# Attentions 1 and 2 of a four-layer decoder: values of both query tiles at once, a pair of jobs later; scores in pieces of 400 columns

## The chip, the cores and the metric

The kernel runs on one core of a Trainium2 chip. The metric is the device time of one execution in microseconds; the table below gives the median of three runs. One execution was also recorded by the hardware profiler, and every duration in this text is read from that record. The engines are TensorE (PE, with its weight loads listed apart as PEld), VectorE (DVE), ScalarE (ACT), GpSimd (POOL) and SyncE (SP, which starts DMAs). Each engine works through its own queue in the order written; engines wait for one another through semaphores.

## The reference

The model takes eight batches of 256 tokens with 128 features, `x`, and for each batch a context of 1601 rows with 64 features. Four layers follow, each a cross attention on the context and a feed-forward block:

```python
x = x + _L0_xattn_ref(_layernorm(x), ctx, ctx, ...)
x = x + _L0_ffn_ref(_layernorm(x), ...)
x = x + _L1_xattn_ref(_layernorm(x), ctx, ...)      # 16 heads of 64
x = x + _L1_ffn_ref(_layernorm(x), ...)
x = x + _L2_xattn_ref(_layernorm(x), ctx, ctx, ...)  # one head
...
scores = jnp.einsum('bhnd,bhmd->bhnm', qh, kh) * scale
attn = jax.nn.softmax(scores, axis=-1)
out = jnp.einsum('bhnm,bhmd->bhnd', attn, vh)
out = out.transpose(0, 2, 1, 3).reshape(B, N, INNER)
return out @ Wo + bo
```

The change touches only the attentions of layers 1 and 2 (counted from 0). Both are computed by one function with the key weights folded into the queries and the value and output weights folded into one matrix per head, so that the context itself, transposed, serves as the keys and, as it is, as the values.

## The kernel before

The function `wide` runs attentions 1 and 2. Its unit is a *job*: one layer and batch, one head `h`, and one tile `j` of 128 queries (0 or 1; `QT` is 2). Attention 1 has 8 batches x 16 heads x 2 tiles = 256 jobs, attention 2 has 8 x 1 x 2 = 16. Jobs 2p and 2p+1 are the two query tiles of one head; this text calls them *pair* p, its even and its odd job.

One job n goes through these steps, with the lines of the profile:

- `scores` (L467): the 128 queries against the 1601 context columns, in four pieces of 512, 512, 512 and 66 columns (65 are used), each piece two matmuls (`qh` and `ql`, the high and low parts of the queries, in the type fp32r). Each piece has its own bank of the accumulator memory PSUM; there are four such banks (`s=4`).
- `maximum` (L474, L477), on VectorE: the maximum of each piece and then of the row. `exponentials` (L488), on ScalarE: four exponentials with sums, which free the four banks, into `e`.
- `turn` (L500, L502): `e` is transposed on TensorE in 13 chunks of 128 columns (the last has 65), four chunks to a turn, into one of two banks (`t=2`), and copied to a tile `pt`. Turns 0 and 1 are copied by ScalarE, turns 2 and 3 by VectorE.
- `values` (L514): 13 fp32 matmuls of the context chunk (64 columns of weights) with the turned chunk (128 moving columns). Even chunks write partitions 0 to 63 of the bank `o` and odd chunks 64 to 127; an fp32 matmul is two instructions in the profile, so 26 are listed a job. There is one bank `o` (`o=1`).
- `take` (L524), on ScalarE, copies the result out, `project` (L528) multiplies it with the output matrix of the head into other columns of the same bank, and `add` (L532), on VectorE, scales it by the inverse sum (`sums`, L519, L520) and adds it to `X[b]`.
- `query` (L438, L443, L444) makes the queries of the next head; it is called in odd jobs.

The order is written out by hand: the body of the loop over n is emitted as it stands, and every engine gets its own instructions in that order. Around job n it is: scores and maxima of job n+1; turns 0 and 1 of job n; project and add of job n-1; now and then a layer norm for a later batch; in odd jobs the queries of the next head; the exponentials of job n+1; turns 2 and 3 of job n; its sums; a step `EARLY` of other work; values and take of job n; a step `LATE` of other work. The other work ("beside") is the feed-forward blocks of layers 0 and 1 for other batches and the preparation of weights, cut into steps of which most jobs get one. `EARLY` issues a step's TensorE, first ScalarE and VectorE parts, `LATE` its other ScalarE and GpSimd parts.

Of the kernel before, what the change touches and what calls it, by code (L numbers as in the profile page):

```python
# [33 lines left out]
F32 = mybir.dt.float32  # L34
F32R = mybir.dt.float32r
AF = mybir.ActivationFunctionType
ALU = mybir.AluOpType
AX = mybir.AxisListType

P = 128  # L40
D = 128
DC = 64
NB = 8
LQ = 256
QT = LQ // P
LK = 1601
NC = (LK + P - 1) // P
LAST = LK - (NC - 1) * P
MAGIC = 12582912.0
TAKEN = -3.0e38  # L50
KW = LK + 1
# [6 lines left out]
def decoder_kernel(ctx: ExitStack, tc: tile.TileContext, a: dict, out: bass.AP):  # L58
    nc = tc.nc
# [18 lines left out]
    def pm():  # L78
        return ps["m"].tile([P, 512], F32, tag="m", name="pm")

    def po():
        return ps["o"].tile([P, 512], F32, tag="o", name="o")
# [63 lines left out]
    X = [const.tile([P, QT, D], F32, tag=f"x{b}", name=f"x{b}") for b in range(NB)]  # L146
# [200 lines left out]
    def run(steps, names):  # L347
        for name in names:
            for step in steps:
                if name in step:  # L350
                    step[name]()
# [38 lines left out]
    def wide(layers, before, extra):  # L390
# [11 lines left out]
        with ExitStack() as es:  # L402
            one = es.enter_context(tc.tile_pool(name="wi1", bufs=1))
            two = es.enter_context(tc.tile_pool(name="wi2", bufs=2))
# [3 lines left out]
            B = [one.tile([P, n, D], F32, name=f"B{l}") for l, (n, _) in enumerate(layers)]  # L408
            bias = {}
            ct, v, y, yT, q, own = {}, {}, {}, {}, {}, {}  # L410

            def load_batch(k):
                ct[k] = two.tile([P, KW], F32R, tag="ct", name="ct")
                nc.sync.dma_start(out=ct[k].bitcast(F32), in_=ctd[k[1]])
                v[k] = two.tile([P, NC, DC], F32, tag="v", name="v")
                load_context(v[k], k[1])
# [6 lines left out]
            def measure(k):  # L423
                stats[k] = deviation(two, k[1])

            def start_batch(k):
                l, b = k
                y[k] = normalise(two, b, *stats[k])
                nc.gpsimd.tensor_tensor(X[b], X[b], layers[l][1][:, None, :].to_broadcast([P, QT, D]), ALU.add)

            def turn_y(k):
                yT[k] = flip_tokens(two, y[k], "yT")
# [24 lines left out]
            jobs = [(k, h, j) for k in keys for h in range(layers[k[0]][0]) for j in range(QT)]  # L457
            st, e, ls, tail = {}, {}, {}, {}

            BANK = [(at, min(512, LK - at)) for at in range(0, LK, 512)]  # L460

            def scores(n, c):
                k, h, j = jobs[n]
                st[n, c] = ps["s"].tile([P, 512], F32, tag="s", name="st")
                at, w = 512 * c, min(512, KW - 512 * c)
                for i in range(2):
                    nc.tensor.matmul(st[n, c][:, 0:w], lhsT=q[k, h][i][:, j * P:(j + 1) * P],  # L467
                                     rhs=ct[k][:, at:at + w], start=(i == 0), stop=(i == 1))

            def maximum(n, c):  # L470

                if c == 0:
                    ls[n] = two.tile([P, 12], F32, tag="ls", name="ls", bufs=3)
                nc.vector.tensor_reduce(ls[n][:, c:c + 1], st[n, c][:, 0:BANK[c][1]], AX.X, ALU.max)  # L474
                if c == 3:
                    shift = ls[n][:, 4:5]
                    nc.vector.tensor_reduce(shift, ls[n][:, 0:4], AX.X, ALU.max, negate=True)  # L477
                    k, _, j = jobs[n]
                    if k[0] in bias:

                        c = own[k][:, j:j + 1]
                        nc.vector.tensor_tensor(shift, shift, c, ALU.subtract)
                        nc.vector.tensor_tensor(shift, shift, c, ALU.add)

            def exponentials(n):
                e[n] = two.tile([P, LK], F32, tag="e", name="e")
                for c, (at, w) in enumerate(BANK):
                    nc.scalar.activation(e[n][:, at:at + w], st[n, c][:, 0:w], AF.Exp, bias=ls[n][:, 4:5], scale=1.0,  # L488
                                         accum_out=ls[n][:, 5 + c:6 + c])

            turned = {}

            def turn(n, i):

                t = ps["t"].tile([P, 512], F32, tag="t", name="t")
                p = turned[n, i] = two.tile([P, 512], F32, tag="pt", name="pt", bufs=5)
                cs = range(4 * i, min(4 * i + 4, NC))
                m = P if cs[-1] < NC - 1 else LAST
                for c in cs:
                    nc.tensor.transpose(t[0:m, (c - 4 * i) * P:(c - 4 * i + 1) * P], e[n][:, c * P:c * P + m], ident)  # L500
                w = P * len(cs)
                (nc.scalar.copy if i < 2 else nc.vector.tensor_copy)(p[0:m, 0:w], t[0:m, 0:w])  # L502

            o = {}

            def values(n, cs):

                k, h, j = jobs[n]
                if cs[0] == 0:
                    o[n] = po()  # L510
                for c in cs:
                    m = P if c < NC - 1 else LAST
                    half = slice(DC * (c % 2), DC * (c % 2) + DC)
                    nc.tensor.matmul(o[n][half, 0:P], lhsT=v[k][0:m, c, :],  # L514
                                     rhs=turned[n, c // 4][0:m, (c % 4) * P:(c % 4 + 1) * P],
                                     start=(c < 2), stop=(c >= NC - 2))

            def sums(n):
                nc.vector.tensor_reduce(ls[n][:, 9:10], ls[n][:, 5:9], AX.X, ALU.add)  # L519
                nc.vector.reciprocal(ls[n][:, 9:10], ls[n][:, 9:10])  # L520

            def take(n):
                tail[n] = two.tile([P, P], F32, tag="os", name="os")
                nc.scalar.copy(tail[n], o[n][:, 0:P])  # L524

            def project(n):
                (l, _), h, j = jobs[n]
                nc.tensor.matmul(o[n][:, P:P + D], lhsT=tail[n], rhs=B[l][:, h, :], start=True, stop=True)  # L528

            def add(n):  # L530
                (_, b), h, j = jobs[n]
                nc.vector.scalar_tensor_tensor(X[b][:, j, :], o[n][:, P:P + D], ls[n][:, 9:10], X[b][:, j, :],  # L532
                                               ALU.mult, ALU.add)

            last = len(jobs) - 1

            loads, measures, starts, turns, ahead = {}, {}, {}, {}, {}
            for n, (k, h, j) in enumerate(jobs):
# [28 lines left out]
            for n, (_, h, j) in enumerate(jobs):  # L567
                more = n < last
                for k in loads.get(n, []):
                    load_batch(k)  # L570
                if more:
                    for c in range(4):
                        scores(n + 1, c)
                        maximum(n + 1, c)
                turn(n, 0)
                turn(n, 1)
                if n:
                    project(n - 1)
                    add(n - 1)
                for k in measures.get(n, []):  # L580
                    measure(k)
                for k in starts.get(n, []):
                    start_batch(k)
                for k in turns.get(n, []):
                    turn_y(k)

                at = n + 2 if n + 2 == first_of_last else n + 3
                if (j == 1 and n + 3 != first_of_last or at == first_of_last != n + 3) and at <= last:
                    for f in query(*jobs[at][0:2]):
                        f()  # L590
                if more:
                    exponentials(n + 1)
                turn(n, 2)
                turn(n, 3)
                sums(n)
                run(beside.get(n, []), EARLY)
                values(n, range(NC))
                take(n)
                run(beside.get(n, []), LATE)
            project(last)  # L600
            add(last)

    def maps1(two, A, B):

# [792 lines left out]
    def ffn1(p, b):  # L1397


        t = {}  # L1400
# [39 lines left out]

        def up(i):
            if i == 0:
                t["h"] = p.tile([P, 4, LQ], F32, name="f1_h")
            t["pt"] = pm()
            for x in range(2):
                nc.tensor.matmul(t["pt"][:, x * LQ:(x + 1) * LQ], lhsT=w1r[:, 2 * i + x, :], rhs=t["yT"],
                                 start=True, stop=True)
# [41 lines left out]

        def take_r(j):  # L1490
            if j == 0:
                t["rT"] = p.tile([P, QT, 512], F32R, name="f1_rT")
            nc.scalar.activation(t["rT"][:, j, :], t["pt"], AF.Identity, bias=magic[:, 1:2], scale=1.0)

        def down():
# [438 lines left out]
```

## Time and profile before

| | |
|---|---|
| median of three runs | 3535.34 us (3530.77 to 3539.50) |
| profiled execution | span 3529.4 us from first to last instruction; its own time around that span is not listed, the three runs lie 1.4 to 10.1 us above the span |
| the stage of `wide` (first to last L467) | 737 to 2450 us of the span |
| PE, DVE, ACT busy in 738 to 2458 | 1632.1, 1209.0, 1130.8 us of 1720 |
| time of one job of attention 1 without other work | 5.40 us (even), 5.70 us (odd) |
| mean over all jobs of attention 1 | 5.92 us (even), 6.46 us (odd) |

The time of a job is read from the starts of its first L467 matmul and that of the next job. In a timeline a line gives start, length, engine, source line, operation, tile written <- tiles read, sizes, count, and in brackets how long the engine was idle before and which work ended the idle time. Lengths of matmuls include the pipeline's latency (0.27 us for 128 columns), so the time a matmul occupies the array is read from the distance of starts. The page's share of busy time does not tell short gaps on TensorE for the same reason.

### The profile page before, as it was taken

Reading aid. Unit: us, or ns where it says so; the run is one execution under the profiler, and the core shown is the slowest. Engines: PE = TensorE matmul, PEld = TensorE weight load, DVE = VectorE, ACT = ScalarE, POOL = GpSimd, SP = SyncE. Lnnn points to the kernel's source line nnn. Section 1 sums busy time; section 2 is a strip of 40 time slices with the busy share of each in tenths; the row PEclk is TensorE's granted clock in tenths of the full one; section 3 lists DMA queues with packets and bytes.
Section 4 is the critical chain, followed back from the end, with each engine's and each line's share of the span. In section 5 each row is a group of like instructions: output and inputs, shape, how many; then the busy total and the mean of one; then the engine's idle time right before and its main releaser. Section 6 shows DMA issues by size and latency. Waiting matters only on the chain.

```text
span 3529.4 us, 75160 instructions
## 1 busy us (share of the span) xinstructions
PE 3380.6 (96%) x28453; PEld 2299.7 (65%) x28453; DVE 2580.6 (73%) x6482; ACT 2290.0 (65%) x5747; POOL 1179.4 (33%) x2105
## 2 busy tenths in 40 slices
PE   7999999989999999999999999988999999999999
PEld 4555555468787877788787878866445555555444
DVE  6888888656776767676776767675557888888665
ACT  3888887746666666667666666654224878787622
POOL 6344344624152513324151520131115333332100
PEclk8999999989999999999999999999998999999999
DMA  5544444120001001000100000021004444443100
GB/s 97 89 73 74 71 77 58 19 83 1 15 1 33 2 1 39 1 15 1 39 1 22 6 1 15 1 66 33 1 0 85 78 63 68 65 69 53 41 5 7
DMA packets 113449, 130.24 MB, mean 37 GB/s; under 512 B 67616, under 2 KB 96832, under 8 KB 112448
## 3 DMA queue, kind: packets, MB, share of 16 engines
q1 hardware_dynamic: 92352, 114.22, 18.0%
q0 software_dynamic: 20480, 10.53, 1.3%
q8 instruction: 225, 3.69, 0.4%
q10 hardware_dynamic: 256, 0.69, 0.1%
q14 instruction: 136, 1.11, 0.1%
HBM read 44.79 MB, written 11.28 MB: 16 GB/s over the span
## 4 chain that ended last, share of the span: by engine, by line
PE 81%; DVE 9%; ACT 6%; POOL 2%; issue 2%; DMA 0%; DVEq 0%; POOLq 0%; SPq 0%; ACTq 0%
PE ov L1081 13%; PE o L514 12%; PE st L467 12%; PE pm L873 11%; PE t L500 8%; PE st L1069 6%; PE gu L1740 3%; PE o L1789 3%; PE gu L1741 3%; ACT pt L502 3%; DVE ls L474 2%; DVE mx L876 2%; ACT e L488 2%; PE st L834 1%; DVE ql L444 1%
## 5 line engine op out<-in xcount | busy, mean ns | idle before, releaser
L876 DVE TENSOR_REDUCE mx<-pm 128x1 f32<-128x512 f32 (+1 forms) x1792 | 1020.3, 627 | 172.7 <-PE pm L873 168.9
L1072 ACT ACTIVATE e<-st 128x512 f32<-128x512 f32 (+1 forms) x1792 | 910.6, 566 | 210.5 <-PE st L1069 160.0
L474 DVE TENSOR_REDUCE ls<-st 128x1 f32<-128x512 f32 x1088 | 549.5, 567 | 292.3 <-PE st L467 291.2
L488 ACT ACTIVATE e<-st,ls 128x512 f32<-128x512 f32 x1088 | 634.0, 602 | 13.4 <-DVE ls L477 12.6
L502 ACT COPY pt<-t 128x512 f32<-128x512 f32 x544 | 293.6, 586 | 460.8 <-PE t L500 459.9
L1081 PE MATMUL ov<-e,V 128*32 128x256 f32 x6656 | 564.6, 392 | 0.3 <-ACT e L1072 0.3
L873 PE MATMUL pm<-K,Q 64*128 64x512 f32 (+1 forms) x2048 | 497.3, 451 | 18.6 <-DVE mx L876 15.4
L500 PE MATMUL t<-ident,e 128*128 128x128 f32 (+1 forms) x3536 | 506.5, 281 | 2.6
L514 PE MATMUL o<-pt,v 128*64 128x128 f32 (+1 forms) x7072 | 490.2, 278 | 17.0 <-DVE pt L502 13.0
L514 PEld LDWEIGHTS o<-pt,v 128*64 128x64 f32 (+1 forms) x7072 | 412.1, 137 | 88.2 <-DVE pt L502 37.2
L873 PEld LDWEIGHTS pm<-K,Q 64*128 64x128 f32 x2048 | 226.1, 187 | 325.8 <-DVE mx L876 223.3
L500 PEld LDWEIGHTS t<-ident,e 128*128 128x128 f32 (+1 forms) x3536 | 391.5, 141 | 52.4 <-ACT pt L502 30.0
L467 PE MATMUL st<-ct,qh 128*128 128x512 f32 x1088 | 406.1, 373 | 1.8 <-ACT e L488 1.8
L1069 PE MATMUL st<-Q,K 64*128 64x256 f32 (+1 forms) x3328 | 403.1, 287 | 0.1
L467 PE MATMUL st<-ct,ql 128*128 128x512 f32 x1088 | 362.9, 367 | 0.0
L1069 PEld LDWEIGHTS st<-Q,K 64*128 64x128 f32 (+1 forms) x3328 | 333.1, 182 | 32.3 <-issue 6.5
L855 POOL DMA_DIRECT2D Q<-qh x256 | 128.3, 501 | 450.5 <-PE st L1069 422.9
L502 DVE COPY pt<-t 128x512 f32<-128x512 f32 (+1 forms) x544 | 239.1, 481 | 34.9 <-PE t L500 34.8
L467 PEld LDWEIGHTS st<-ct,qh 128*128 128x128 f32 x1088 | 205.6, 189 | 86.3 <-issue 34.9
L1081 PEld LDWEIGHTS ov<-e,V 128*32 128x32 f32 x6656 | 142.5, 108 | 153.7 <-issue 37.9
L1742 ACT ACTIVATE act<-gu 128x512 f32<-128x512 f32 x130 | 77.5, 597 | 243.2 <-PE gu L1741 232.1
L488 ACT ACTIVATION_READ_ACCUMULATOR e<-st,ls 128x1 f32 x1088 | 230.7, 212 | 0.0
(545 smaller groups left out, 4302.2 us busy)
## 6 DMA issues: line engine op xcount, KB each, us to landing
K<-kh SPq DMA_DIRECT2D x250, 100.1 KB
K<-kl SPq DMA_DIRECT2D x250, 100.1 KB
ct<-ctd SPq DMA_DIRECT2D x23, 801.0 KB
ctd<-ct SPq DMA_DIRECT2D x8, 801.0 KB
v<-in_ctx SPq DMA_DIRECT2D x16, 384.0 KB
Q<-qh POOLq DMA_DIRECT2D x256, 16.0 KB, 2.7
Q<-ql POOLq DMA_DIRECT2D x256, 16.0 KB, 3.0
raw<-in_ctx SPq DMA_DIRECT2D x8, 384.0 KB
```

The costliest lines, as they stand in the source:

```text
L467: nc.tensor.matmul(st[n, c][:, 0:w], lhsT=q[k, h][i][:, j * P:(j + 1) * P], rhs=ct[k][:, at:at + w], start=(i == 0), stop=(i == 1))
L474: nc.vector.tensor_reduce(ls[n][:, c:c + 1], st[n, c][:, 0:BANK[c][1]], AX.X, ALU.max)
L488: nc.scalar.activation(e[n][:, at:at + w], st[n, c][:, 0:w], AF.Exp, bias=ls[n][:, 4:5], scale=1.0, accum_out=ls[n][:, 5 + c:6 + c])
L500: nc.tensor.transpose(t[0:m, (c - 4 * i) * P:(c - 4 * i + 1) * P], e[n][:, c * P:c * P + m], ident)
L502: (nc.scalar.copy if i < 2 else nc.vector.tensor_copy)(p[0:m, 0:w], t[0:m, 0:w])
L514: nc.tensor.matmul(o[n][half, 0:P], lhsT=v[k][0:m, c, :], rhs=turned[n, c // 4][0:m, (c % 4) * P:(c % 4 + 1) * P], start=(c < 2), stop=(c ...
L855: nc.gpsimd.dma_start(out=q[r:P:8, :].bitcast(F32), in_=qhl[b][r % 2][src, :].bitcast(F32))
L873: nc.tensor.matmul(pt[g][:, x * w:(x + 1) * w], lhsT=q[r, j * P:(j + 1) * P], rhs=k[r, at:at + w], start=True, stop=True)
L876: nc.vector.tensor_reduce(mx[:, js[0]:js[-1] + 1, 2 * t + g, at // 512], pt[g][:, 0:len(js) * w].rearrange("p (j k) -> p j k", k=w), AX.X, ...
L1069: nc.tensor.matmul(st[g][0:m, j, :], lhsT=k[r, c * P:c * P + m], rhs=q[r, :], start=True, stop=True)
L1072: nc.scalar.activation(e[0:m, 2 * t + g, 0:len(cs), :], st[g][0:m, 0:len(cs), :], AF.Exp)
L1081: nc.tensor.matmul(cell["o"][32 * g:32 * g + 32, :], lhsT=v[0:m, at:at + 32], rhs=e[0:m, g, c % 2, :], start=(c == 0), stop=(c == NC - 1))
```

## The change

1. `scores` uses pieces of 400, 400, 400 and 401 columns (402 in the matmul).
2. `turn` writes both tiles of a pair side by side: the tile `pt` holds, for each chunk, 128 columns of the even and 128 of the odd job.
3. `values` works on a pair: one matmul with 256 moving columns for each of chunks 0 to 11, and for chunk 12 (65 rows) two of 128, one for each tile, the first into partitions 0 to 63 and the second into 64 to 127. Chunks 0 to 5 of pair p-1 are issued in the even job of pair p, the other seven in the odd job, between turns 1 and 2. In attention 2 (and for the last pair of attention 1) all of them are issued in the odd job of the pair itself, where they stood before.
4. `take` copies 256 columns, once a pair. `project` does both tiles and now holds the two adds; in attention 1 it is issued in the even job, two pairs later, ahead of turns 0 and 1 and behind the maxima.
5. `ls` has 8 buffers, `pt` five of twice the size and `pt3` two; in the feed-forward block of layer 1 `f1_rT` shares the memory of `f1_h`.

```diff
-            BANK = [(at, min(512, LK - at)) for at in range(0, LK, 512)]
+            BANK = [(400 * c, 400 if c < 3 else LK - 1200) for c in range(4)]
...
-                p = turned[n, i] = two.tile([P, 512], F32, tag="pt", name="pt", bufs=5)
+                if j == 0:
+                    turned[p, i] = two.tile([P, len(cs), QT, P], F32, tag="pt" if i < 3 else "pt3", name="pt",
+                                            bufs=5 if i < 3 else 2)
...
-                (nc.scalar.copy if i < 2 else nc.vector.tensor_copy)(p[0:m, 0:w], t[0:m, 0:w])
+                (nc.scalar.copy if i < 2 else nc.vector.tensor_copy)(
+                    turned[p, i][0:m, :, j, :], t[0:m, 0:P * len(cs)].rearrange("p (c q) -> p c q", q=P))
...
+            HALVES = (0, 1, 2, 3, 4, 5), (6, 7, 8, 9, NC - 1, 10, 11)
+            def values(p, cs):
+                k, h, _ = jobs[QT * p]
                 if cs[0] == 0:
-                    o[n] = po()
+                    o[p] = po()
                 for c in cs:
...
+                    if c == NC - 1:
+                        for j in range(QT):
+                            nc.tensor.matmul(o[p][DC * j:DC * j + DC, j * P:(j + 1) * P], lhsT=v[k][0:LAST, c, :],
+                                             rhs=turned[p, c // 4][0:LAST, 0, j, :], start=False, stop=False)
+                    else:
+                        half = slice(DC * (c % 2), DC * (c % 2) + DC)
+                        nc.tensor.matmul(o[p][half, 0:LQ], lhsT=v[k][:, c, :],
+                                         rhs=turned[p, c // 4][:, c % 4, :, :].rearrange("p j q -> p (j q)"),
+                                         start=(c < 2), stop=(c >= NC - 3))
...
+            def project(p):
+                (l, b), h, _ = jobs[QT * p]
+                for j in range(QT):
+                    nc.tensor.matmul(o[p][:, LQ + j * P:LQ + j * P + D], lhsT=tail[p][:, j * P:(j + 1) * P],
+                                     rhs=B[l][:, h, :], start=True, stop=True)
+                for j in range(QT):
+                    nc.vector.scalar_tensor_tensor(X[b][:, j, :], o[p][:, LQ + j * P:LQ + j * P + D],
+                                                   ls[QT * p + j][:, 9:10], X[b][:, j, :], ALU.mult, ALU.add)
...
+                p = n // QT
+                if j == 0 and 2 <= p <= now:
+                    project(p - 2)
                 turn(n, 0)
                 turn(n, 1)
-                if n:
-                    project(n - 1)
-                    add(n - 1)
+                if j == 0 and p > now:
+                    project(p - 1)
...
                 if more:
                     exponentials(n + 1)
+                if 1 <= p <= now:
+                    values(p - 1, HALVES[j])
+                    if j == 1:
+                        take(p - 1)
+                        if p == now:
+                            project(p - 1)
                 turn(n, 2)
                 turn(n, 3)
                 sums(n)
                 run(beside.get(n, []), EARLY)
-                values(n, range(NC))
-                take(n)
+                if p >= now and j == 1:
+                    values(p, HALVES[0] + HALVES[1])
+                    take(p)
                 run(beside.get(n, []), LATE)
```

`now` is the number of the last pair of attention 1 (127).

More of the change, by code (lines that the diff above doesn't have):

```diff
@@ L464, in scores @@
                 st[n, c] = ps["s"].tile([P, 512], F32, tag="s", name="st")
-                at, w = 512 * c, min(512, KW - 512 * c)
+                at, w = BANK[c]
+                w += w % 2
                 for i in range(2):
@@ L472, in maximum @@
                 if c == 0:
-                    ls[n] = two.tile([P, 12], F32, tag="ls", name="ls", bufs=3)
+                    ls[n] = two.tile([P, 12], F32, tag="ls", name="ls", bufs=8)
                 nc.vector.tensor_reduce(ls[n][:, c:c + 1], st[n, c][:, 0:BANK[c][1]], AX.X, ALU.max)
@@ L493, in turn @@
             def turn(n, i):
+                p, j = divmod(n, QT)
+                cs = range(4 * i, min(4 * i + 4, NC))
                 t = ps["t"].tile([P, 512], F32, tag="t", name="t")
-                p = turned[n, i] = two.tile([P, 512], F32, tag="pt", name="pt", bufs=5)
-                cs = range(4 * i, min(4 * i + 4, NC))
+                if j == 0:
+                    turned[p, i] = two.tile([P, len(cs), QT, P], F32, tag="pt" if i < 3 else "pt3", name="pt",
+                                            bufs=5 if i < 3 else 2)
                 m = P if cs[-1] < NC - 1 else LAST
@@ L500, in turn @@
                     nc.tensor.transpose(t[0:m, (c - 4 * i) * P:(c - 4 * i + 1) * P], e[n][:, c * P:c * P + m], ident)
-                w = P * len(cs)
-                (nc.scalar.copy if i < 2 else nc.vector.tensor_copy)(p[0:m, 0:w], t[0:m, 0:w])
+                (nc.scalar.copy if i < 2 else nc.vector.tensor_copy)(
+                    turned[p, i][0:m, :, j, :], t[0:m, 0:P * len(cs)].rearrange("p (c q) -> p c q", q=P))
             o = {}
-            def values(n, cs):
-                k, h, j = jobs[n]
+            HALVES = (0, 1, 2, 3, 4, 5), (6, 7, 8, 9, NC - 1, 10, 11)
+            def values(p, cs):
+                k, h, _ = jobs[QT * p]
                 if cs[0] == 0:
-                    o[n] = po()
+                    o[p] = po()
                 for c in cs:
[L512 to L516, printed above, removed]
+                    if c == NC - 1:
[7 more added lines that the diff above has]
+                                         start=(c < 2), stop=(c >= NC - 3))
             def sums(n):
@@ L520, in sums, with take @@
                 nc.vector.reciprocal(ls[n][:, 9:10], ls[n][:, 9:10])
[L522 to L533, printed above, removed]
+            def take(p):
+                tail[p] = two.tile([P, LQ], F32, tag="os", name="os")
+                nc.scalar.copy(tail[p], o[p][:, 0:LQ])
+            def project(p):
[6 more added lines that the diff above has]
+                                                   ls[QT * p + j][:, 9:10], X[b][:, j, :], ALU.mult, ALU.add)
             last = len(jobs) - 1
+            now = layers[0][0] * NB - 1
             loads, measures, starts, turns, ahead = {}, {}, {}, {}, {}
@@ L596, in wide @@
                 run(beside.get(n, []), EARLY)
-                values(n, range(NC))
-                take(n)
+                if p >= now and j == 1:
+                    values(p, HALVES[0] + HALVES[1])
+                    take(p)
                 run(beside.get(n, []), LATE)
-            project(last)
-            add(last)
+            project(last // QT)
     def maps1(two, A, B):
@@ L1442, in up @@
             if i == 0:
-                t["h"] = p.tile([P, 4, LQ], F32, name="f1_h")
+                t["h"] = p.tile([P, 4, LQ], F32, tag="f1_h", name="f1_h")
             t["pt"] = pm()
@@ L1491, in take_r @@
             if j == 0:
-                t["rT"] = p.tile([P, QT, 512], F32R, name="f1_rT")
+                t["rT"] = p.tile([P, QT, 512], F32R, tag="f1_h", name="f1_rT")
             nc.scalar.activation(t["rT"][:, j, :], t["pt"], AF.Identity, bias=magic[:, 1:2], scale=1.0)
```

## The prediction

> **What bounds the kernel now.** First the page: its span, its busy shares and its slices say where to look.
>
> ```profile
> span 3529.4 us, 75160 instructions
> PE 3380.6 (96%) x28453; PEld 2299.7 (65%) x28453; DVE 2580.6 (73%) x6482; ACT 2290.0 (65%) x5747; POOL 1179.4 (33%) x2105
> ...
> PEclk8999999989999999999999999999998999999999
> ...
> PE 81%; DVE 9%; ACT 6%; POOL 2%; issue 2%; DMA 0%; DVEq 0%; POOLq 0%; SPq 0%; ACTq 0%
> ```
>
> TensorE is busy almost throughout, also in the stage of the change (737 to 2450 us), at a clock near 1, and holds 81% of the chain that ended last. So fewer TensorE cycles are worth their time, if nothing else becomes late. Who might is told by the waits of that stage:
>
> ```profile
> ACT pt L502 <- PE t L500: 459.9, 272, 3.2
> DVE ls L474 <- PE st L467: 291.2, 237, 4.2
> ...
> PE o L514 <- DVE x L532: 4.0, 7, 0.6
> ```
>
> VectorE sat idle before the first maximum of a job 237 times, 1.23 us a time: that is all the slack it has behind TensorE. The last line shows that values waits for the add, since there is one bank `o`; today it costs 4 us in all. Last, the timeline of a job without other work:
>
> ```profile
> 2270.32 0.16 DVE L477 TENSOR_REDUCE ls<-ls 128x1 f32<-128x4 f32 x1
> 2270.47 0.62 PEld L500 LDWEIGHTS t<-ident,e 128*128 128x128 f32 x5 [0.21 <-ACT pt L502]
> 2270.47 0.81 PE L500 MATMUL t<-ident,e 128*128 128x128 f32 x5
> 2270.49 0.35 DVE L532 SCALAR_TENSOR_TENSOR x<-o,ls,x 128x128 f32<-128x128 f32 x1
> ...
> 2271.16 0.89 DVE L502 COPY pt<-t 128x512 f32<-128x512 f32 x2 [0.32 <-PE t L500]
> ...
> 2271.22 1.75 PE L514 MATMUL o<-pt,v 128*64 128x128 f32 x26
> ...
> 2271.97 0.14 DVE L519 TENSOR_REDUCE ls<-ls 128x1 f32<-128x4 f32 x1
> ...
> 2272.15 0.17 DVE L520 RECIPROCAL ls<-ls 128x1 f32<-128x1 f32 x1
> ...
> 2272.89 0.49 PE L467 MATMUL st<-ct,qh 128*128 128x512 f32 x1
> ...
> 2273.66 2.02 DVE L474 TENSOR_REDUCE ls<-st 128x1 f32<-128x512 f32 x4 [1.34 <-PE st L467]
> ...
> 2274.53 1.09 PE L500 MATMUL t<-ident,e 128*128 128x128 f32 x8
> ```
>
> See what values covers: from 2271.22 to 2272.89, 1.67 us, TensorE works on it while VectorE copies turns 2 and 3 and makes the sums, done at 2272.32, 1.85 us after the first transpose of turn 2. VectorE then waits 1.34 us for the next scores. Less than 1.67: without values there, VectorE is late.
>
> **The change part by part, on a pair without other work.** Before it takes 5.40 + 5.70 = 11.10 us.
>
> *Scores.* The 512-column matmuls start 0.235 us apart, the last two (66 columns) take 0.14 together (2274.39 to 2274.53), the first loses 0.10 after values. Eight of 400 columns at 0.235 x 400/512 take 1.47, and I give 0.04 at the start: 1.51 against 1.64. The saving lies between 0.04 (if 0.02 of the 0.235 is a fixed cost) and 0.17 a job; I take 0.13, for the 66-column pair is the row that shows a floor. A pair: 0.26.
>
> *Values.* Matmuls of the two column halves run side by side: two of 128 columns every 0.109 us, and the last chunk, alone, 0.23. So 12 x 0.109 + 0.23 = 1.54 a job. The query matmuls (L438, 256 columns) start 0.217 apart, so six new chunks take 1.30; chunk 12 fills both halves and takes 0.23 a pair. 3.08 becomes 2.83: 0.25 saved. Bounds: nothing (the L1081 matmuls of 256 columns start in groups 0.24 apart) and 0.25. Entering and leaving the halves (0.10 to 0.15 and 0.15 to 0.20) happens as often as before.
>
> A rule speaks for much more. The Trainium skill, TensorEngine Tiling, Instruction Overhead, says that each matmul carries about 60 cycles of overhead. Estimated from that page, 24 instructions fewer a pair would save 0.6 us, 76 us over 127 pairs, and the sum below would end near no change. The trace differs: the 66-column matmuls start 0.03 us apart, and doubling the columns doubles the distance.
>
> *Gaps on TensorE.* The wait of turn 2 for a bank (0.21, even job) and of values for VectorE's copy (0.19, odd job) are filled by values of the pair before: 0.27 of their 0.40 saved, the rest is what TensorE loses anyway at a change of work. Project has four matmuls of 0.11 as before. So TensorE alone would need 11.08 - 0.78 = 10.30: 5.05 even, 5.25 odd.
>
> *ScalarE.* One take of 256 columns (0.37, as L443) for two of 0.27; exponentials and copies move as many elements in as many instructions. Its exponentials would start 3.6 us into a job, after the copies of turns 0 and 1, and end 2.3 later, at 5.9; the last bank is wanted at 6.2 or later. Hidden, with 0.3 to spare. The copies' strided output has no row: between nothing and some tenths, which that spare covers in most jobs. Nothing is issued on POOL or SP.
>
> *VectorE.* The maxima stay at 2.02 and 0.21 with the shift. The two adds (L532, 0.35 each; L1308 and L1504 show such pairs at 0.74 and 0.59; I take 0.68) now come in the even job directly behind the maxima, and behind them, in VectorE's queue, the copies of turns 2 and 3. The first matmul of values, chunk 0, starts in the same job a new bank `o`: in the changed program's order it waits for the second add, in 127 pairs. Behind it on TensorE stand turns 2 and 3 and the next scores: all wait.
>
> This makes a loop. From the first transpose of turn 2 in the odd job: VectorE free at 1.85; maxima, shift, adds and 0.05 to the release: 2.96, so values starts at 4.81. From there values 1.35, leaving 0.15, turns 2 and 3 0.55: the odd job's scores start at 6.86. Scores 1.51, turns 0 and 1 0.93, query 0.43, entering 0.10, values 1.30 + 0.23 + 0.04, leaving 0.15: 4.69. Round: 11.55, against 11.10 before. TensorE waits 1.2 us a pair in front of values, more than the 0.78 saved. What values covered was VectorE's backlog; now VectorE starts the maxima 1.25 us after the scores instead of 0.77, and the adds stand behind.
>
> *With other work.* Mean pair before: 5.92 + 6.46 = 12.38. Other TensorE work and its stalls, read as the extra between the first transpose of turn 2 and the start of values, is 0.51 in even and 0.77 in odd jobs. In odd jobs it now lies inside the wait and costs nothing; in even jobs it stays, 0.51. VectorE becomes free on average 2.87 us after turn 2 starts in odd jobs (126 of them), not 1.85, with its share of the other work. Of this 0.2 goes, since `ql` (L444, 0.42) will be done long before turn 2: 2.65. The round is 2.65 + 9.70 + 0.51 = 12.86, 0.48 more. Bounds: 2.40 (stalls behind `ql` go too) gives +0.23, 2.87 gives +0.70. Over 127 pairs: +61 us, from +29 to +89; the bounds of scores and values add -10 to +45.
>
> *Attention 2* (8 pairs, 126 us) is set by chains of the last batch's feed-forward steps; even jobs lose their values, odd jobs hold them all. By its row of 5.40 to 10.66 us a job I see no sign: 0, within 10. The shared memory `f1_h` costs nothing: its last reader (job +14) is on TensorE a job ahead of `f1_rT` (+15).
>
> Sum: 3529.4 + 61 = 3590, and 5.9 more as the median stands above the span: 3596.
>
> **Rivals.**
> 1. *The wait stays short.* If VectorE's share of the other work found gaps, so that it is free at the plain 1.85 in all jobs, the round is 12.06: -0.32 x 127 = -41, 3494. It decides at 2.17, where the round equals 12.38. For: steps vary much, many jobs have no VectorE step. Against: the mean of 2.87 is measured, and nothing of it is removed but `ql`.
> 2. *No wait:* the add is done in time, TensorE alone sets the pair: 10.30 + 0.51 + about 0.5 = 11.31, -136, 3400. Against: the adds cannot end before maxima that start 0.62 us after the scores, so at 3.5, when TensorE arrives at 3.0.
> 3. *The backlog spreads.* In a few jobs of each batch VectorE is late by 2 to 4 us (L1461, L1308, which wait for ScalarE's steps behind the exponentials). Late maxima in odd jobs then delay the exponentials and the four banks. With 2.87 and 0.25 more a pair: +120, 3655.
> 4. *Both cancel*, within 10 us, which is about 0.3%, what a measurement of this kernel can tell from no change.
>
> **How the numbers follow.** The forecast (3560 to 3630) has 0.5, rival 3 0.21, rival 1 0.16, rival 2 0.06, rival 4 0.07. Slower: 0.71; same: 0.07; faster: 0.22. The predicted time is the forecast's, 3596. For 8 in 10 the range leaves out rival 2 and the ends of rivals 1 and 3: 3490 to 3655.
>
> **What would show it.** Right: the first values matmul of a pair waits for L541, about 127 times and some 1.2 us each; scores start to start about 5.3 odd and 6.2 even without other work; VectorE's wait for scores almost gone; values' matmuls 0.22 us apart in pairs; the stage some 60 us longer. Wrong: if that wait is under 0.7 us on average, or if the 400-column pieces or 256-column matmuls run at another distance than their rows say, above all if they gain the overhead that I left out.

## The result and the profile after

The changed kernel takes 3573.1 us (median of 4 runs, 3569.2 to 3580.3), the kernel before 3537.4 on the same chip: ratio 1.0102, 95% interval 1.0082 to 1.0123. It is 36 us slower, on the forecast side, where 61 had been worked out.

The page of the changed kernel answers the lines shown of before: span, busy time, the chain that ended last, and two of the costliest groups (busy time, mean ns | idle time of the engine before them and what ended most of it).

```profile
span 3567.5 us, 68510 instructions
PE 3299.1 (92%) x25189; PEld 2160.8 (61%) x25189; DVE 2546.8 (71%) x6482; ACT 2269.0 (64%) x5611; POOL 1176.2 (33%) x2105
...
PE 73%; DVE 21%; ACT 3%; issue 2%; POOL 1%; DMA 0%; DVEq 0%; POOLq 0%; ACTq 0%; SPq 0%
...
L523 PE MATMUL o<-pt,v 128*64 128x256 f32 x3264 | 448.5, 398 | 152.0 <-DVE x L541 148.6
L475 DVE TENSOR_REDUCE ls<-st 128x1 f32<-128x400 f32 x1088 | 546.1, 564 | 29.3 <-PE st L468 28.3
```

TensorE is busy 81.5 us less, and the span is 38.1 us longer. VectorE's share of the chain went from 9% to 21%. The list of waits of the stage (us in total, times, longest) names the place:

```profile
DVE pt L505 <- PE t L504: 413.5, 253, 4.0
...
PE o L523 <- DVE x L541: 148.6, 126, 3.6
...
DVE ls L475 <- PE st L468: 28.3, 12, 8.4
```

Before, the first of these waits was small:

```profile
DVE pt L502 <- PE t L500: 34.8, 105, 1.6
```

Values (L523) waits 126 times, 1.18 us a time, for the second add (L541). Before, VectorE waited for scores, 291 us; that slack is down to 28. VectorE is not busy all the time even so: it now waits 413.5 us for turns 2 and 3 (L504), which TensorE reaches only behind values. The two engines wait for each other in turn. The chain in a pair without other work shows the round (start, length, what):

```profile
2267.43 0.88 DVE pt L505 x2
2268.32 0.08 DVE ls L528
...
2268.58 1.93 DVE ls L475 x4
...
2270.61 0.62 DVE x L541 x2
...
2271.27 1.52 PE o L523 x12
2272.79 0.69 PE t L504 x5
2273.49 1.46 PE st L468 x8
2274.94 0.87 PE t L504 x8
2275.81 0.43 PE pm L438 x2
...
2277.92 0.60 PE t L504 x4
...
2278.54 0.88 DVE pt L505 x2
```

Read it as a circle: VectorE's copies, sums, four maxima and two adds, then TensorE's first half of values, turns 2 and 3, scores, turns, queries, second half of values, turn 2, and VectorE's copies again. From copy to copy it takes 11.11 us: the time of the pair. TensorE alone would need about 10.1, since it stands idle 0.99 us of it, as the timeline of the next round has it:

```profile
2279.60 2.00 DVE L475 TENSOR_REDUCE ls<-st 128x1 f32<-128x400 f32 x4
...
2281.72 0.61 DVE L541 SCALAR_TENSOR_TENSOR x<-o,ls,x 128x128 f32<-128x128 f32 x2
...
2282.38 0.65 PE L523 MATMUL o<-pt,v 128*64 128x256 f32 x4 [0.99 <-DVE x L541]
```

The scores of that job started at 2278.37, so the maxima start 1.23 us behind them, not 0.77 as before: VectorE was still at the copies of turns 2 and 3, which nothing covers any more. There is no idle time in brackets ahead of L475.

Where the 38.1 us of the span came from, by the starts of the scores: 4.2 before the first scores (737.5 to 741.7; that point lies between 737.8 and 746.2 in the runs below, none of which changes anything ahead of it), -3.3 in the first three jobs, whose values are put off, +20.2 in the other jobs of attention 1 (the mean pair went from 12.38 to 12.54), +15.2 from the scores of job 255 to those of job 271, that is the last job of attention 1 and attention 2 (132.4 to 147.6), +1.8 behind. The recorded expectations below call this stretch the part from job 256 on; it starts one job earlier. Between the scores of jobs 256 and 271 alone it is 15.8 (125.8 to 141.6).

In attention 2 the even jobs have no values at all. This is TensorE from the turns of an odd job of the first pair on:

```profile
2361.89 1.04 PE L504 MATMUL t<-ident,e 128*128 128x128 f32 x8
2362.76 0.38 PE L257 MATMUL pm<-ident,ln_y 128*128 128x128 f32 x2
2366.28 0.70 PE L438 MATMUL pm<-yT,A 128*128 128x256 f32 x2 [3.14 <-DVE yT L260]
```

And this is what VectorE did meanwhile:

```profile
2361.02 0.88 DVE L505 COPY pt<-t 128x512 f32<-128x512 f32 x2
...
2363.31 2.00 DVE L475 TENSOR_REDUCE ls<-st 128x1 f32<-128x400 f32 x4
...
2365.81 0.42 DVE L260 COPY yT<-pm 128x256 f32<-128x256 f32 x1
```

The even job was over after 4.1 us; its copies, a layer norm and the sums were still in VectorE's queue when the next scores had long been made (2359.68), so the maxima started 3.6 us behind them. The copy `yT`, which the queries need, stands behind the maxima: TensorE idles 3.14 us.

That idle time is the smaller part of the loss. These are attention 2 in the changed kernel and in the kernel before (from, to, length, then busy time and instructions of PE, PEld, DVE, ACT and POOL, the mean granted clock of TensorE, and the share and GB/s of the DMA engines):

```profile
2342.70:2486.00 143.30, 115.65 (x701) 88.15 (x700) 90.34 (x321) 64.40 (x179) 34.95 (x113) 0.86 0.20 55
2322.10:2450.00 127.90, 105.02 (x850) 87.03 (x850) 89.11 (x316) 64.91 (x186) 34.36 (x109) 0.95 0.22 62
```

The stretch is 15.4 us longer. TensorE's idle time grew by 4.8 us of it, from 22.9 to 27.7; its busy time grew by 10.6, with fewer matmuls, at a lower clock. Behind the idle 3.14 us the clock is 0.64 (2366 to 2370), and the five transposes there take 1.31 us (2367.22) where they take 0.77 in the pair above (2277.85).

### The profile page after: what moved, and what is told of

The parts are those of the page before. It is cut to its first block, busy times and chain, and to the rows that moved or that the text cites. A ratio compares the mean times of both kernels' runs of the same rounds, so it can differ in the third digit from the quotient of the medians.

```text
span 3567.5 us, 68510 instructions
## 1 busy us (share of the span) xinstructions
PE 3299.1 (92%) x25189; PEld 2160.8 (61%) x25189; DVE 2546.8 (71%) x6482; ACT 2269.0 (64%) x5611; POOL 1176.2 (33%) x2105
## 4 chain that ended last, share of the span: by engine, by line
PE 73%; DVE 21%; ACT 3%; issue 2%; POOL 1%; DMA 0%; DVEq 0%; POOLq 0%; ACTq 0%; SPq 0%
PE ov L1100 13%; PE o L523 11%; PE pm L892 10%; DVE ls L475 8%; PE t L504 7%; PE st L1088 6%; PE st L468 5%; PE o L1808 3%; PE gu L1759 3%; PE gu L1760 3%; DVE pt L505 3%; DVE x L541 2%; PE pm L438 2%; DVE mx L895 2%; PE st L853 1%
## 5 line engine op out<-in xcount | busy, mean ns | idle before, releaser
L489 ACT ACTIVATE e<-st,ls 128x400 f32<-128x400 f32 x1088 | 634.5, 604 | 72.6 <-DVE ls L478 71.3
L523 PE MATMUL o<-pt,v 128*64 128x256 f32 x3264 | 448.5, 398 | 152.0 <-DVE x L541 148.6
L475 DVE TENSOR_REDUCE ls<-st 128x1 f32<-128x400 f32 x1088 | 546.1, 564 | 29.3 <-PE st L468 28.3
L504 PE MATMUL t<-ident,e 128*128 128x128 f32 (+1 forms) x3536 | 497.0, 279 | 1.6 <-DVE pt L505 0.9
L504 PEld LDWEIGHTS t<-ident,e 128*128 128x128 f32 (+1 forms) x3536 | 401.0, 142 | 110.6 <-ACT e L489 63.4
L468 PE MATMUL st<-ct,qh 128*128 128x400 f32 x1088 | 420.3, 386 | 4.9 <-ACT e L489 4.4
L523 PEld LDWEIGHTS o<-pt,v 128*64 128x64 f32 x3264 | 211.9, 140 | 292.0 <-DVE x L541 178.3
L468 PE MATMUL st<-ct,ql 128*128 128x400 f32 x1088 | 380.5, 350 | 0.0
```

Of the source, the lines that this page charges most:

```text
L523: nc.tensor.matmul(o[p][half, 0:LQ], lhsT=v[k][:, c, :], rhs=turned[p, c // 4][:, c % 4, :, :].rearrange("p j q -> p (j q)"), start=(c < 2 ...
```

## The experiments

All times are medians; ratios are to the kernel before on the same chip (median 3539.4 for e1 to e4, 3539.7 for e5 to e8). Differences to the changed kernel compare measurements taken apart from each other; the kernel before differs by some 2 us between them. "Attention 1" is the time from the scores of job 3 to those of job 255.

**e1, the pieces alone.** The kernel before with the new pieces only:

```diff
-            BANK = [(at, min(512, LK - at)) for at in range(0, LK, 512)]
+            BANK = [(400 * c, 400 if c < 3 else LK - 1200) for c in range(4)]
...
-                at, w = 512 * c, min(512, KW - 512 * c)
+                at, w = BANK[c]
+                w += w % 2
```

> The kernel before with nothing changed but the pieces of the scores (400, 400, 400, 401). If TensorE sets the time of a job, the job is shorter by what eight matmuls of 400 columns save: in the changed kernel they start 0.180 us apart and take 1.54 us with the transposes behind them, before 1.64, so 0.10 x 272 = 27 us, 3510. Rival: if the jobs with other work are set by waits on VectorE or ScalarE, only the plain third of the jobs gains: 9 us, 3528.

3511.4 us, ratio 0.9921 (0.9904 to 0.9938). All of the 27 us came: jobs without other work went from 5.70 and 5.40 to 5.58 and 5.26, the mean pair to 12.19. This part of the change is a gain by itself, in the jobs with other work too.

**e2, values where it stood.** The changed kernel with values of the pair before behind turns 2 and 3, the sums and the early step (`pt` has one buffer more, `os` one in all, and two tiles of the feed-forward block share memory):

```diff
-                if 1 <= p <= now:
-                    values(p - 1, HALVES[j])
-                    ...
                 turn(n, 2)
                 turn(n, 3)
                 sums(n)
                 run(beside.get(n, []), EARLY)
+                if 1 <= p <= now:
+                    values(p - 1, HALVES[j])
+                    ...
```

> The changed kernel with values of the pair before issued where values stood before, behind turns 2 and 3, the sums and the early step of other work (pt has six buffers; os has one and f1_y and f1_yT share memory to make room). Theory of the backlog: VectorE copies turns 2 and 3 beside values again, the maxima start 0.7 us after the scores, the adds end before values begins, and the wait for them (149 us) is gone; the wait of turn 2 for its bank comes back (0.3 us in even jobs). A plain pair falls from 11.11 to about 10.65 us, the kernel to 3573 - 60 = 3513 or less. Rival: the pairing itself is what costs (256-column matmuls, strided copies, adds in twos): the time stays at 3560 to 3580.

3524.3 us, ratio 0.9960 (0.9945 to 0.9976): 49 us under the changed kernel, but 11 over the 3513 expected. The list of waits of that kernel (us in total, times, longest) shows VectorE's slack back and the wait for the adds gone, as the theory of the backlog has it:

```profile
DVE ls L475 <- PE st L468: 246.7, 217, 6.7
...
PE t L504 <- ACT pt L505: 30.9, 129, 0.2
...
PE o L523 <- DVE x L541: 6.8, 8, 0.9
```

So place, not pairing, made the wait. A pair without other work takes 10.71, as expected, but the mean pair 12.17, only 0.02 under e1, and attention 2 keeps its loss (145.0 us from the scores of job 255 on). Set against e1, pairing in the old place brings nothing with other work about. Why the gain of 0.13 in plain pairs is gone there was not followed further.

**e3, the adds between the maxima.** The changed kernel with project and its adds of attention 1 behind the second of the four maxima:

```diff
                     for c in range(4):
+                        if c == 2 and j == 0 and 2 <= n // QT <= now:
+                            project(n // QT - 2)
                         scores(n + 1, c)
                         maximum(n + 1, c)
                 p = n // QT
-                if j == 0 and 2 <= p <= now:
-                    project(p - 2)
```

> The changed kernel with project and its two adds of attention 1 issued between the second and the third piece of the next scores and maxima. Theory: the adds then stand behind two maxima, not four, and end 1 us earlier; values no longer waits for them (149 us to under 30), project waits up to 0.3 us for the take, and the maxima end 0.6 us later, which delays the exponentials in even jobs. A plain pair takes 10.5 us, the kernel 3500 to 3520. Rival: TensorE then waits as long for the exponentials' banks, and the time stays at 3560 to 3580.

3479.4 us, ratio 0.9831 (0.9809 to 0.9852): 94 us under the changed kernel, more than expected. The same work, the same place of values; two instructions of VectorE and four of TensorE stand earlier in their queues. The waits of TensorE in it:

```profile
PE o L523 <- DVE x L541: 23.6, 25, 2.0
...
PE o L538 <- ACT os L533: 12.7, 29, 1.5
```

The wait for the adds fell by 125 us; the wait of project for the take costs 13, and ScalarE's wait for the maxima rose from 71 to 84. A pair without other work takes 10.57. The rival, that TensorE would then wait as long for the banks, falls: scores wait 3.6 us for the exponentials, 4.4 in the changed kernel.

**e4 and e8, the same dose in both kernels.** One more VectorE reduction of 400 columns, its result unused, ahead of the adds in even jobs of the changed kernel (e4) and ahead of the add in even jobs of the kernel before (e8):

```diff
+                if p + 2 <= now:
+                    n = QT * (p + 2)
+                    nc.vector.tensor_reduce(ls[n][:, 10:11], e[n][:, 0:400], AX.X, ALU.max)
```

```diff
+                if j == 1 and n + 1 < last:
+                    nc.vector.tensor_reduce(ls[n + 1][:, 10:11], e[n + 1][:, 0:400], AX.X, ALU.max)
```

> The changed kernel with one more VectorE reduction of 400 columns (0.5 us, its result unused) ahead of the two adds in 126 even jobs. If the loop over VectorE sets the pair, all of it is paid: +0.5 x 126 = 63 us, 3636, and the wait of values for the adds grows from 149 to about 210 us. Rival: if the wait has slack behind it (TensorE would wait for the banks anyway), less than half: under 3600.

> The kernel before with the same additional VectorE reduction of 400 columns (0.5 us) ahead of the add in the even jobs. Theory: VectorE has 1.2 us of slack behind TensorE there, so it costs nothing in plain jobs and little in the few where VectorE is late: 3540 to 3550. Rival: VectorE's time counts in this stage as much as in the changed kernel (additional 71 us): 3600 and more.

e4: 3644.5 us, ratio 1.0297 (1.0279 to 1.0315), 71 above the changed kernel. e8: 3546.5 us, ratio 1.0021 (1.0011 to 1.0031), 7 above the kernel before. The view of its line in e4 (shortest, median and longest in ns, first and last start) gives its length, 0.558 us:

```profile
L542 DVE TENSOR_REDUCE ls<-e x126: 558/558/561, 775.5 to 2424.7; 128x1 f32<-128x400 f32 x126
```

So 126 x 0.558 = 70 us of VectorE were paid in full in the changed kernel, and of 135 x 0.558 = 75 us in the kernel before a tenth. The wait of values for the adds grew from 148.6 to 209.0. In the profiled executions attention 1 grew by 80 us (1580.5 to 1660.7) by the dose, and by 12 in the kernel before, so "in full" holds to some 10 us. This settles what sets the pair: VectorE's time between the copies and the adds, about one for one.

**e5, attention 2 by tiles.** The changed kernel with values, take and project of attention 2 one tile at a time, as before, from the new layout (`values1` and `project1` are the old functions):

```diff
-                if j == 0 and p > now:
+                if j == 0 and p == now + 1:
                     project(p - 1)
+                elif p > now:
+                    project1(n - 1)
...
-                if p >= now and j == 1:
+                if p == now and j == 1:
                     values(p, HALVES[0] + HALVES[1])
                     take(p)
+                elif p > now:
+                    values1(n)
```

> The changed kernel, with values, take and project of attention 2 alone as before, one tile at a time in every job, read from the new layout. Theory: the 15 us that attention 2 took longer come from its even jobs without values, where nothing covers VectorE's backlog; the part from the first scores of job 256 to the last falls from 147.6 back to 132 to 134 us, the kernel to 3558 to 3562. Rival: that part is set by the chains of the last batch's feed-forward steps and by adds two tiles at a time, whatever the order of values: 145 to 148 us, 3573.

3556.6 us, ratio 1.0050 (1.0032 to 1.0067). The part from the scores of job 255 on fell from 147.6 to 136.8, not to the 132 to 134 expected: the order of values accounts for 11 of the 15 us. The rest lies between the scores of jobs 256 and 257, 12.9 us where it was 7.7 before: the last pair of attention 1 still ends there, with both its halves, and nothing was undone about that. The gain shows in TensorE's busy time more than in its waits: in attention 2 it is busy 106.5 us (115.7 in the changed kernel) at a clock of 0.94, and idle 25.9 (27.7).

**e6 and e7, both mends.** e5 with the adds behind the second maximum (`c == 2`, e6) or the third (`c == 3`, e7).

> Both mends together: the adds of attention 1 behind the second of the four maxima, and attention 2 by tiles as before. If the two costs are apart, their gains add: 3479 for the adds, less 10 for attention 2, 3469, against 3540 of the kernel before. Rival: the adds' mend already took attention 2's loss (142.8 us there): 3479.

> As the two mends together, but with project and the adds behind the third of the four maxima. A maximum takes 0.5 us, so the adds end 0.5 later and values would wait 0.3 to 0.4 us for them in even jobs, but project no longer waits for the take (0.2). If the end of the adds sets the pair, 20 to 45 us slower than behind the second: 3490 to 3512. Rival: the take's wait weighs as much: 3465 to 3475.

e6: 3471.2 us, ratio 0.9806 (0.9788 to 0.9824), the fastest of all, 1.9% under the kernel before. That is within 2 us of the 3469 expected, but the two gains do not quite add: e3 gave 94 us and e5 16.5, both together 102. The part from the scores of job 255 on, 142.8 in e3 already, fell only to 138.2, so the rival holds in part. e7: 3479.0 us, ratio 0.9833 (0.9812 to 0.9854). Here neither expectation was met: the wait for the adds rose from 23 to 62 us, the one for the take fell from 12.6 to 3.9, and attention 1 took 1503.8 instead of 1490.7 us, so the end of the adds counts, but the intervals of the two totals overlap.

## Why the prediction was right or wrong

*What bounds the kernel, and the new wait:* right. VectorE's 1.23 us of slack was the row that decided. With values taken from behind turn 2, the maxima start 1.23 us behind the scores (1.25 predicted), the first matmul of a pair waits for the second add 126 times (127), 1.18 us in the mean and 0.99 in the plain pair shown (1.2). e2, e3, e4 and e8 show the cause by place, order and dose.

*Scores:* 0.13 a job predicted for a plain pair; e1 has 0.12 and 0.14 there, and 0.10 as the mean of all jobs.

*Values:* right. The pairs of 256-column matmuls start 0.216 apart (0.217), chunk 12 takes 0.22 (0.23). The rule of the Trainium skill weighed against the rows, TensorEngine Tiling, Instruction Overhead, some 60 cycles a matmul, taken as a cost that each matmul adds, does not show here: 128 columns took 0.109 and 256 took 0.216, twice as much, although 24 instructions fewer are issued a pair.

*The round:* this is the term that was mis-sized. 11.55 was predicted for a plain pair, 11.11 measured: 4.81 from turn 2 to values became 4.53 (2277.85 to 2282.38), 6.74 for the rest 6.58. Of the 0.28, 0.10 lies ahead of the maxima, which start while the sums are still ending (1.75 us after turn 2, not 1.85), and the shift and the two adds end 0.73 us behind the maxima where 0.89 was put down (0.21 and 0.68): I added lengths of instructions that overlap in the record. The smaller half, 0.16, are rounding and gaps that I counted around TensorE's groups. 0.44 a pair is 56 us over 127 pairs, of a net effect of 61. A plain pair did not become longer at all (11.10 before). The sum for TensorE alone starts from 11.08, where the parts give 11.10; nothing hangs on it.

*Other work:* 1.31 was put on the plain pair, 1.43 measured (12.54 less 11.11). The step that TensorE's other work in odd jobs disappears in the wait is borne out by the starts: in pairs 2 to 125, whatever TensorE did in between, values starts 0.05 us behind the end of the second add. On average the maxima start 2.46 us after turn 2 where 2.65 was put down, and values 5.23 where it was 5.61; the rest of the pair takes 7.3, as predicted (7.25). So the miss lies in VectorE's part of the round. In all attention 1 lost 20 us instead of 61.

*Attention 2:* wrong. I saw no sign of a loss and put 0, within 10; it was 15. The sign was in my own argument: even jobs "lose their values", and that values covers VectorE's copies I had just shown for attention 1. e5 gave 11 of it back. The prediction had no term for the clock, and most of the 15 us shows as TensorE at a lower clock.

*The total:* 36 us came out where 61 were predicted, and part of that is luck. Without the 15 us of attention 2, which were not foreseen, the time would have been some 3558, just below the forecast's 3560 to 3630.

*Rivals:* 1 (the wait stays short) and 2 (no wait) fall with the 126 waits; 3 (the backlog spreads) too: ScalarE's wait for the maxima is 71 us in all, and scores wait only 4.4 us for the banks (6 times); 4 (both cancel) was nearest in size, within 0.02 us in plain pairs, by the loss and the gain that the forecast names.

## What to carry to other kernels

Work that is moved away from a place leaves behind whatever it covered there: before moving it, list which engine was catching up beside it, and how much slack that engine had (here 1.67 us of cover against 1.23 to 1.34 of slack). Where two engines hand work to and fro, add up the whole round from a point back to the same point, by starts and not by lengths, and compare it with what the busiest engine needs alone; the dose test (a useless 0.56 us instruction) tells in one run whether the round binds. And where an engine late in a round holds up a scarce buffer, look first at the order in its own queue: two adds moved ahead of two maxima turned 1.0% slower into 1.7% faster, and e6 into 1.9%.

## What was not expected of the hardware

The matmuls of 400 columns in fp32r start 0.180 us apart and those of 512 0.235, that is 0.45 and 0.46 ns a column, without a fixed cost to be seen; the 66-column pair, 0.14 instead of 0.06, was the one that did not follow, and even pieces avoid it. In attention 2 the mean granted clock of the stretch was 0.95 before, 0.86 in the changed kernel, 0.94 in e5 and 0.91 in e6. It does not follow the share of idle time: TensorE is idle 19% of it in the changed kernel and 20% in e5. It goes with single long gaps. From job 256 on TensorE has four gaps of over 2.3 us in the changed kernel (2.34 to 3.22), two before (2.46 and 4.68) and two in e5 (2.65 and 4.68), and in the 3 us behind each of these eight the clock was 0.50 to 0.65; in e3 one gap of 2.70 had 1.00 behind it. Behind gaps of 1.4 to 2.1 us the clock lay anywhere between 0.50 and 1.00. No run changed the gaps alone, so how much of the 15 us the clock cost is not shown apart from the order.
